# Graph attention on one Trainium2 core: key and value rows fetched one by one from the SyncE queue, 16 in three groups out of four in place of 8 in each group

## The chip, the cores and the metric

The kernel runs on one core of a Trainium2 chip. Time is device microseconds (us) of one execution. The core has five engines with an instruction stream each: TensorE (PE in the profile, PEld for its weight loads), VectorE (DVE), ScalarE (ACT), GpSimd (POOL) and SyncE (SP). SP computes nothing here: it issues DMAs. Data lie in HBM, in SBUF (128 partitions) and in PSUM, where TensorE writes.

## The reference

One graph-attention layer with residuals and two normalizations, N = 12,500 nodes, E = 212,500 edges sorted by their destination, width 128, 8 heads of 16:

```
Q, K, V = x @ WQ, x @ WK, x @ WV
Eh = edge_attr @ WE
score = exp(clip(sum over a head of (K[src] * Q[dst] / 4 * Eh), -5, 5))
wV = segment_sum(V[src] * score, dst);  Z = segment_sum(score, dst)
h = x + wV / (Z + 1e-6)
h = (h - mean over nodes) * rsqrt(var + 1e-5) * gamma + beta
out = layernorm(x + h) over the 128 columns
```

The source of an edge is random, so `K[src]` and `V[src]` are rows fetched from anywhere in a table. The destinations rise, so `Q[dst]` and the sums over a destination work on windows of 64 neighbouring nodes.

## The kernel before

**Table.** A first stage (L590 to L610, some 100 us) multiplies x by WK and WV and writes the rows of the table `kvd` to HBM: one row a node, 256 numbers (K, then V), 1 KB.

**Main loop.** The edges are cut into 1661 tiles of 128, and these into 208 groups of eight tiles (two windows of four; the last group has five). Iteration g of the loop at L671 holds steps for several groups at once, in an order written by hand. DVE runs `products` (L520, K times a projected edge feature), `both` (L503), `scores` (L527), `attn` (L570), `turned_onehot` (L461), `message` (L539, V times the score) and `onehot` (L451, L453, L454); TensorE runs the edge projection `ehqe` (L490 reads the tile `ea`, L498 follows), transposes (L511, L576) and the sums (L554); ScalarE moves PSUM results (L492, L534, L559, L582).

**How rows of the table arrive.** For each group a slot of eight tiles is filled by gathers (`gather`, L198, L199): an indirect DMA on POOL fetches 128 rows of `kvd`, one per partition, by a column of indices `srcs`. There are eight slots. When `message` has used a slot, `load_kv` (L234) gives it to a later group and appends that group's gathers to the list `queued`; all but seven go out at once, and `pace` (L206) puts one behind each of the marked DVE steps (L454, L520, the two L503, L527, L570), which POOL then waits for.

**Row loads.** In some groups the eighth tile isn't gathered by POOL. Its 128 rows come by 128 DMAs of 1 KB each from SP into a tile `byrow` (two buffers), which `products` and `message` then read in an instruction of its own (`parts`, L222). `row_groups` (L55) chooses the groups, `fill` (L216 to L219) gives each a run of successive loop iterations, and in each of these `fetch_rows` (L225) loads that many row indices from the tile `row_ids` into SP's registers (L228) and issues that many row DMAs (L232). With ROWS = 8 it takes 16 iterations for a tile, the last one three iterations (ROW_LAG) ahead of the group, and 12 tiles are filled back to back, in iterations 5 to 196.

**SP's queue.** SP executes its DMAs in order. In iteration g it issues:

```
within(load, g + 4)        # ea: 512 KB of edge features, three buffers (L420)
within(load_rel, g + 5)    # rb: two DMAs of 64 KB, three buffers (L346)
if g in fill:
    fetch_rows(*fill[g])   # L228, then L232 once for each row
```

`ea` of group g + 4 is used by `ehqe` (L490) in iteration g + 2, and `rb` of g + 5 by `turned_onehot` (L461) in iteration g + 2. The completions of SP's DMAs are counted on eight semaphores in turn, so a DMA can wait for the one eight places before it. Loads of x for the last stage (L407) follow on the same queue when the gathers have ended.

**Last stage** (L743 on): normalization, second residual and layernorm of all nodes, some 90 us.

Of the kernel before, what the change touches and what calls it, by code (L numbers as in the profile page):

```python
# [10 lines left out]
I32 = mybir.dt.int32  # L11
# [3 lines left out]
ET = mybir.EngineType  # L15

P = 128
# [4 lines left out]
U = 4  # L22
# [3 lines left out]
NX = 8  # L26
EARLY = 4
RUN = 64
ROWS = 8
FIRST_ROW = 5  # L30
ROW_LAG = 3


LAST = [3, 2]
# [2 lines left out]
def plan(N, T):  # L37

    n, r = divmod(T - sum(LAST), U)
    sizes = [U] * n + [r] * (r > 0) + list(LAST)  # L40
    assert n > 1 and len(sizes) % 2 == 0
    starts = [sum(sizes[:g]) for g in range(len(sizes))]
    cuts = list(range(0, N - 64, CH)) + [N - 64, N]
    due = {}
    thr = [0.0] * len(sizes)
    for j, c in enumerate(cuts[1:]):
        need = (c + (64 if c < N - CH else 24)) * T
        g = next((g for g, t in enumerate(starts) if t * N >= need), None)
        if g is not None:
            due.setdefault(g, []).append(j)  # L50
            thr[g] = float(c)
    return sizes, starts, cuts, due, thr


def row_groups(sizes):  # L55


    span = P // ROWS + ROW_LAG
    return [2 * g for g in range(max(FIRST_ROW + span, NX), sizes.count(U) // 2, P // ROWS)]


@with_exitstack
def gnn_kernel(
# [19 lines left out]
    nc = tc.nc  # L83
    N, D = out.shape
    T = src.shape[1]
    NW = dstb.shape[1]
    usizes, ustarts, cuts, due, _ = plan(N, T)
    NG = NW // 2
    sizes = [usizes[2 * g] + usizes[2 * g + 1] for g in range(NG)]
# [5 lines left out]
    consts = ctx.enter_context(tc.tile_pool(name="consts", bufs=1))  # L95
# [46 lines left out]
    def load_rest():  # L142
        nc.scalar.dma_start(base_i, bass.AP(tensor=dstb.tensor, offset=dstb.offset, ap=[[0, P], [1, NW]]))
        nc.scalar.dma_start(rel_i[:, :cut], dst[:, :cut])
        nc.scalar.dma_start(row_ids, rsrc)
        nc.scalar.dma_start(w_q, wq)
        nc.scalar.dma_start(w_e, we)
        nc.scalar.dma_start(srcs[:, nxg * G:cut], src[:, nxg * G:cut])
# [64 lines left out]


    by_row = {w // 2: None for w in row_groups(usizes)}
    fill = {}  # L216
    for k, g in enumerate(by_row):
        for i in range(P // ROWS):
            fill[g - ROW_LAG - P // ROWS + i] = (g, k, i)  # L219
    row_ids = consts.tile([P // ROWS, len(by_row) * ROWS], I32, name="row_ids")  # L220

    def parts(g, a, b):  # L222
        return [(a, b - 1), (b - 1, b)] if g in by_row and b == G else [(a, b)]
# [1 line left out]
    def fetch_rows(g, k, i):  # L225
        if i == 0:
            by_row[g] = rows.tile([P, 1, 2 * P], F32, name="byrow", bufs=2)
        _, ids = nc.values_load_multi_w_load_instructions(  # L228
            row_ids[i:i + 1, k * ROWS:(k + 1) * ROWS], engines=(ET.SP,), min_val=0, max_val=N - 1,
            skip_runtime_bounds_check_because="node ids")  # L230
        for p, r in enumerate(ids, i * ROWS):
            nc.sync.dma_start(by_row[g][p:p + 1, 0, :], kvd[ds(r, 1), :])  # L232
# [396 lines left out]
    for q in range(NQ):  # L629
        load_xT((q + 5) * 4 * P)  # L630
        if q == 2:
            load_rest()
        for g, a in piece.get(q, []):
            if a == 0:
                i = free.pop(0)
                kv_view(g, (i, slot(i)))
            turn_x(g, a)
        table_rows(4 * q)
        for g, a in piece.get(q, []):
            project(g, a, wide)  # L640
        k = q - first_step
        if 0 <= k < len(steps):
            for f, *a in steps[k]:
                f(*a)
# [26 lines left out]
    for g in range(NG):  # L671
        within(load, g + 4)
        within(load_rel, g + 5)
        if g in fill:
            fetch_rows(*fill[g])
# [241 lines left out]
def lay_out(x, src, dst, edge_attr_128, L0_gnn_WQ, L0_gnn_WK, L0_gnn_WV, L0_gnn_WE, L0_gnn_bn_gamma,  # L917
# [12 lines left out]

    sp = tiles(src, 0)
    rsrc = [sp[:, starts[g] + G - 1].reshape(P // ROWS, ROWS) for g in row_groups(sizes)]
    eaT = np.zeros((P, T * P), np.float32)
    eaT[:, :E] = ea.T
# [31 lines left out]
```

## Time and profile before

| | before |
|---|---|
| median of 9 runs (lowest, highest) | 2810.48 us (2788.47, 2825.11) |
| profiled execution: time, span | 2809.55 us, 2807.6 us |
| granted TensorE clock, mean of the span | 0.811 |
| busy: PE, DVE, POOL, ACT | 1923.2, 1648.9, 1588.4, 650.4 us |
| gathers of `kvd` on POOL (L199) | 1585 |
| row DMAs on SP (L232), in groups of eight (L228) | 1536, 192 |
| loads of `ea`, of `rb` | 208, 416 |
| HBM read, written | 364.57 MB, 19.63 MB |

The profile is of one execution on the chip. "busy" is the time in which an engine executes; issuing a DMA isn't counted, so SP has no busy time, and its instructions are seen in a timeline of its queue (SPq). A group of the page is a source line with its engine, operation and tiles: how often, busy us in all, mean ns of one, then the idle time of the engine ahead of it and what ended most of that. "issue" means that the engine waited for nothing the profile shows, "remote" that the semaphore's writer isn't seen. In a timeline each line is start, length, engine, source line and tiles, with the idle time before it in brackets.

### The profile page before, as it was taken

How to read it: one execution, taken by the hardware profiler on the slowest of the kernel's cores; microseconds unless marked ns; L12 is line 12 of the kernel's file. 1: busy time of each engine (PE TensorE's matmuls, PEld its weight loads, DVE VectorE, ACT ScalarE, POOL GpSimd, SP SyncE). 2: the span in 40 equal slices, each digit the busy share in tenths (PEclk: the TensorE clock that was granted, in tenths of full speed). 3: DMA queues.
4: the chain of work that ended last, by engine and by line, in shares of the span. 5: the costliest groups of instructions: out<-in, count | busy, mean ns of one | idle time of the engine just before them, and what ended most of it. 6: DMA issues, size and time to landing. Idle time of an engine off the chain costs nothing. (4 is left out here: it accounts for less than half of the span.)

```text
span 2807.6 us, 37902 instructions
## 1 busy us (share of the span) xinstructions
PE 1923.2 (68%) x9350; PEld 1264.5 (45%) x9350; DVE 1648.9 (59%) x3571; ACT 650.4 (23%) x2509; POOL 1588.4 (57%) x1681
## 2 busy tenths in 40 slices
PE   7577676766677676766665766766676766676687
PEld 5355444544344444544333434444444534444455
DVE  3346556655565666656555655656565656566585
ACT  2133222212222222222121221222222212222225
POOL 5645565655555565655554655556555655656524
PEclk9889788878877787788887878787878777878797
DMA  7644444444444444444444444444444444444453
GB/s 236 215 126 126 130 125 136 134 134 130 131 138 149 135 128 140 141 124 139 127 128 130 133 126 140 130 131 140 130 137 122 141 135 128 142 133 137 136 174 95
DMA packets 179740, 386.86 MB, mean 138 GB/s; under 512 B 41838, under 2 KB 96151, under 8 KB 179511
## 3 DMA queue, kind: packets, MB, share of 16 engines
q0 software_dynamic: 78128, 212.05, 25.9%
q1 hardware_dynamic: 98038, 169.83, 20.1%
q10 hardware_dynamic: 3345, 2.48, 0.3%
q8 instruction: 77, 1.26, 0.2%
q14 instruction: 152, 1.25, 0.1%
HBM read 364.57 MB, written 19.63 MB: 137 GB/s over the span
## 5 line engine op out<-in xcount | busy, mean ns | idle before, releaser
L199 POOL DMA_INDIRECT slot<-kvd,srcs x1585 | 1498.9, 946 | 1087.9 <-issue 330.7
L554 PE MATMUL ps_a<-msg,oh 128*128 128x136 f32 (+1 forms) x3322 | 672.1, 351 | 54.5 <-issue 52.7
L554 PEld LDWEIGHTS ps_a<-msg,oh 128*128 128x128 f32 (+1 forms) x3322 | 548.1, 212 | 159.1 <-issue 144.4
L490 PE MATMUL ps_e<-ea,w_e 128*128 128x512 f32 x832 | 455.7, 666 | 130.5 <-issue 68.4
L576 PE MATMUL ps_m<-ident,at 128*128 128x128 f32 x416 | 123.5, 388 | 461.7 <-DVE oh L454 363.9
L451 DVE TENSOR_TENSOR oh<-ps_m,rel_i 128x512 f32<-128x512 f32 x208 | 142.9, 687 | 501.1 <-remote 415.5
L520 DVE TENSOR_TENSOR p<-slot,ps_t 128x512 f32<-128x512 f32 (+1 forms) x408 | 259.5, 674 | 145.6 <-remote 119.4
L576 PEld LDWEIGHTS ps_m<-ident,at 128*128 128x128 f32 x416 | 80.4, 242 | 562.4 <-ACT xw L440 387.0
L503 DVE TENSOR_TENSOR wt<-wt,ps_q 128x512 f32<-128x512 f32 x416 | 266.1, 679 | 83.0 <-remote 54.2
L492 ACT ACTIVATE wt<-ps_e 128x512 f32<-128x512 f32 x416 | 228.0, 587 | 286.0 <-remote 184.9
L511 PE MATMUL ps_t<-ident,wt 128*128 128x128 f32 x1661 | 246.7, 294 | 67.4 <-DVE wt L503 48.3
L490 PEld LDWEIGHTS ps_e<-ea,w_e 128*128 128x128 f32 x832 | 160.6, 214 | 256.2 <-issue 228.4
L534 ACT ACTIVATE ps_m<-s 128x64 f32<-128x64 f32 x208 | 47.3, 228 | 953.6 <-issue 225.1
L527 DVE TENSOR_REDUCE s<-p 128x64 f32<-128x1024 f32 x208 | 251.3, 1208 | 0.0
L511 PEld LDWEIGHTS ps_t<-ident,wt 128*128 128x128 f32 x1661 | 207.4, 152 | 85.3 <-DVE wt L503 62.9
L539 DVE TENSOR_TENSOR msg<-slot,ps_m 128x1024 f32<-128x1024 f32 (+1 forms) x204 | 244.4, 1198 | 1.6 <-ACT hx L582 1.4
L498 PE MATMUL ps_q<-ot,q 64*128 64x512 bf16 x1248 | 201.8, 410 | 61.3 <-issue 60.3
L559 ACT ACTIVATE os<-ps_a 128x136 f32<-128x136 f32 x208 | 58.5, 281 | 708.8 <-remote 553.2
L498 PEld LDWEIGHTS <-q 64*128 64x128 bf16 x1248 | 49.6, 97 | 285.8 <-issue 260.5
L479 DVE SCALAR_TENSOR_TENSOR qr<-ps_m,q 128x128 f32<-128x128 f32 x208 | 58.2, 280 | 179.9 <-ACT hx L582 141.6
L471 PE MATMUL ps_m<-w_q,xw 128*128 128x128 f32 x416 | 107.3, 351 | 23.8 <-DVE oh L454 23.0
L461 DVE TENSOR_SCALAR ot<-rb,wiota 128x512 bf16<-128x512 bf16 x207 | 80.5, 389 | 65.4 <-DMA rb<-relT 60.8
(111 smaller groups left out, 1672.3 us busy)
## 6 DMA issues: line engine op xcount, KB each, us to landing
ea<-eaT SPq DMA_DIRECT2D x207, 512.0 KB
rb<-relT SPq DMA_DIRECT2D x414, 64.0 KB
slot<-kvd,srcs POOLq DMA_INDIRECT x1585
byrow<-kvd SPq DMA_DIRECT2D x1536, 1.0 KB
kvd<-t SPq DMA_DIRECT2D x24, 512.0 KB
slot<-xT SPq DMA_DIRECT2D x24, 256.0 KB
out<-o SPq DMA_DIRECT2D x24, 256.0 KB
hx<-xT SPq DMA_DIRECT2D x11, 512.0 KB
```

The source lines that it names most:

```text
L199: return nc.gpsimd.indirect_dma_start(out=out, out_offset=None, in_=table, in_offset=bass.IndirectOffsetOnAxis(ap=srcs[:, e:e + 1], axis=0))
L451: nc.vector.tensor_tensor(one, iota_ps[:, None, :].to_broadcast([P, n, P]), r[:, :n, None].to_broadcast([P, n, P]), op=OP.is_equal)
L490: nc.tensor.matmul(eh, w_e, EA[g][:, a:b, :].rearrange("p a b -> p (a b)"), start=True, stop=True)
L492: nc.scalar.activation(t[:, :(b - a) * P], eh, AF.Copy)
L498: nc.tensor.matmul(QE[g][h], Q3[g][r, k, :], OT[g][r, :(b - a) * P], start=(k == 0), stop=(k == 2))
L503: pace(nc.vector.tensor_tensor(t, t, QE[g][h], op=OP.mult))
L511: nc.tensor.transpose(ps[:, j, :], WT[g][h][:, j * P:(j + 1) * P], ident)
L520: step = nc.vector.tensor_tensor(PR[g][:, c:d, :], KV[g](c, d, 0), PW[g][i][:, c - a:d - a, :], op=OP.mult)
L527: pace(nc.vector.tensor_reduce(SS[g][:, :n, :], PR[g][:, :n, :].rearrange("p t (h d) -> p t h d", d=DH), axis=AX.X, op=OP.add))
L539: nc.vector.tensor_tensor(MSG[g][:, a:b, :P].rearrange("p t (h d) -> p t h d", d=DH), KV[g](a, b, P).rearrange("p t (h d) -> p t h d", d=D ...
L554: nc.tensor.matmul(AGG[g][WN if j >= n else 0:], OH[g][j], MSG[g][:, j, :], start=(j == 0), stop=(j == n - 1))
L576: nc.tensor.matmul(ps, AT[g], ident, start=True, stop=False)
```

## The change

A step now issues 16 row DMAs in place of 8, in three iterations out of four, so a tile takes eight steps. `row_steps` lists the iterations; tiles take them eight at a time, and a tile's group is three iterations after its last step. This gives 18 tiles (groups 17, 28, 38, ... 188, 198) in place of 12 (groups 24, 40, ... 200), filled in iterations 5 to 195. The row indices of 18 tiles would make rows of 288 numbers; they are folded into 24 partitions of 96, so that the tile `row_ids` keeps its width.

```diff
-ROWS = 8
+ROWS = 16
 FIRST_ROW = 5
 ROW_LAG = 3
+ROW_REST = 4
...
+def row_steps(sizes):
+    return [g for g in range(FIRST_ROW, sizes.count(U) // 2) if (g - FIRST_ROW) % ROW_REST != ROW_REST - 1]
...
 def row_groups(sizes):
-    span = P // ROWS + ROW_LAG
-    return [2 * g for g in range(max(FIRST_ROW + span, NX), sizes.count(U) // 2, P // ROWS)]
+    ends = row_steps(sizes)[P // ROWS - 1::P // ROWS]
+    return [2 * max(g + ROW_LAG, NX) for g in ends if max(g + ROW_LAG, NX) < sizes.count(U) // 2]
...
-        nc.scalar.dma_start(row_ids, rsrc)
+        nc.scalar.dma_start(row_ids, rsrc.rearrange("i (a r) -> (i a) r", a=fold))
...
+    steps_of_rows = row_steps(usizes)
     fill = {}
     for k, g in enumerate(by_row):
         for i in range(P // ROWS):
-            fill[g - ROW_LAG - P // ROWS + i] = (g, k, i)
-    row_ids = consts.tile([P // ROWS, len(by_row) * ROWS], I32, name="row_ids")
+            fill[steps_of_rows[k * (P // ROWS) + i]] = (g, k, i)
+    fold = next(a for a in (5, 4, 3, 2, 1) if len(by_row) % a == 0)
+    each = len(by_row) // fold
+    row_ids = consts.tile([P // ROWS * fold, each * ROWS], I32, name="row_ids")
...
-            row_ids[i:i + 1, k * ROWS:(k + 1) * ROWS], engines=(ET.SP,), min_val=0, max_val=N - 1,
+            row_ids[i * fold + k // each:i * fold + k // each + 1, k % each * ROWS:(k % each + 1) * ROWS], engines=(ET.SP,), min_val=0, max_val=N - 1,
```

## The prediction

> **What bounds the kernel now.** I read the page first, for the costly groups and the releasers. No engine is full: PE is busy for 68% of the span, DVE for 59%, POOL for 57%.
>
> ```profile
> L199 POOL DMA_INDIRECT slot<-kvd,srcs x1585 | 1498.9, 946 | 1087.9 <-issue 330.7
> ...
> L451 DVE TENSOR_TENSOR oh<-ps_m,rel_i 128x512 f32<-128x512 f32 x208 | 142.9, 687 | 501.1 <-remote 415.5
> ```
>
> A gather takes POOL 0.946 us, and DVE loses some 2 us a group ahead of L451 to a releaser that the profile can only call "remote". So the second view is the timeline of POOL, and then of DVE, over a stretch in mid-loop (start, length, engine, line).
>
> ```profile
> 1102.00 0.94 POOL L199 DMA_INDIRECT slot<-kvd,srcs  x1 [2.62 <-DVE oh L454]
> ...
> 1110.75 0.95 POOL L199 DMA_INDIRECT slot<-kvd,srcs  x1 [0.30 <-issue]
> 1115.22 0.94 POOL L199 DMA_INDIRECT slot<-kvd,srcs  x1 [3.52 <-DVE oh L454]
> ```
>
> ```profile
> 1106.92 1.20 DVE L539 TENSOR_TENSOR msg<-slot,ps_m 128x1024 f32<-128x1024 f32 x1
> 1113.67 0.69 DVE L451 TENSOR_TENSOR oh<-ps_m,rel_i 128x512 f32<-128x512 f32 x1 [5.54 <-remote]
> ```
>
> Eight gathers follow each other every 1.25 us (0.95 and a gap of 0.30), from 1102.0 to 1112.0. DVE is held from 1108.1 to 1113.67, and ACT's L559 is released at 1113.67 as well: 1.7 us after the last gather was issued. Then L454 lets the next gathers go at 1115.22. The cycle is 8 x 1.25 + 1.7 + 1.5 = 13.2 us. I call the stretch in which a run of gathers holds the others **the hold**. It needs no row loads: between 120 and 140 us, before the first row load, 15 gathers run and DVE is busy for 0.2 us.
>
> The third view is SP's own timeline, since SP issues the rows: first where nothing holds it, then in the cycle above.
>
> ```profile
> 1502.49 3.16 SPq L232 DMA_DIRECT2D byrow<-kvd  x8
> 1505.74 0.36 SPq L420 DMA_DIRECT2D ea<-eaT  x1
> 1506.20 1.10 SPq L346 DMA_DIRECT2D rb<-relT  x2
> 1508.51 3.15 SPq L232 DMA_DIRECT2D byrow<-kvd  x8
> ```
>
> ```profile
> 1104.38 9.97 SPq L232 DMA_DIRECT2D byrow<-kvd  x8
> 1114.45 0.36 SPq L420 DMA_DIRECT2D ea<-eaT  x1
> 1114.90 1.10 SPq L346 DMA_DIRECT2D rb<-relT  x2
> 1117.21 9.82 SPq L232 DMA_DIRECT2D byrow<-kvd  x8
> ```
>
> A free step of SP (row ids, eight rows, ea, two rb) takes 1508.51 - 1502.49 = 6.02 us. In the held cycle the same step takes 1117.21 - 1104.38 = 12.83 us, because the eight rows take 9.97 us in place of 3.16. The fourth view is what SP waits for between 190 and 2662 us (us in total, times, longest).
>
> ```profile
> SPq L420 <- PE ps_e L490: 16.7, 6, 8.9
> SPq L232 <- DMA byrow<-kvd: 15.5, 36, 0.8
> SPq L346 <- DMA relT<-relrow: 12.2, 1, 12.2
> ```
>
> All its waits there add up to 94.6 us, of which 22.4 us are at L232 (a lane or an earlier load) and 72 us for buffers of ea and rb. The loads of row ids run from 190.3 to 2656.1 us, 192 times: 2465.8 / 191 = 12.91 us for a step. So SP, though it computes nothing, works for 96% of the loop; 6.02 us of a step is work, 0.50 us waiting and 6.39 us loss to the hold. It is sometimes late already, by the waits of all engines:
>
> ```profile
> PE ps_e L490 <- DMA ea<-eaT: 61.7, 14, 10.5
> DVE ot L461 <- DMA rb<-relT: 60.8, 13, 11.0
> ```
>
> The reader is to see two limits side by side: a run of gathers makes the cycle about 13 us, and SP needs 12.91 us for its step.
>
> **The change, part by part.** *Gathers.* By the built order of instructions 18 groups have seven gathers in place of 12: 1585 - 6 = 1579. Each is worth 1.25 us of a run if the run sets the cycle: 6 x 1.25 = 7.5 us gained. If SP sets it, the gain goes into POOL's idle time. I take 0 for my forecast and 7.5 us for the first rival.
>
> *DVE.* Six more groups split products and message. From the rows by form: products 548 + 280 in place of 679 ns, message 1073 + 276 in place of 1208 ns, together 0.29 us a group, 1.7 us in all, hidden in the holds (5.54 us above); 1.7 us if that cover goes.
>
> *Row loads.* 18 x 128 = 2304 in place of 1536, so 768 more, in 144 steps of 16 in place of 192 steps of eight. Eight rows take 3.16 us where nothing holds SP: (3.16 - 0.23) / 7 = 0.42 us a row (its two register instructions and the 0.228 us of the median DMA).
>
> ```profile
> L232 SPq DMA_DIRECT2D byrow<-kvd x1536: 2/228/1421, 191.5 to 2662.2; - x192
> ```
>
> A load of row ids has a median of 0.976 us, 1.03 with its gap, and there are 48 fewer. Free work added: 768 x 0.42 - 48 x 1.03 = 322.6 - 49.4 = 273 us, over the same groups (steps 5 to 195 in place of 5 to 196). What is moved: in iteration g the queue has ea of group g + 4, rb of g + 5, then the rows; so 16 rows stand ahead of the next ea and rb, 3.4 us more even when free, and PE (L490) and DVE (L461) wait for those. The rows themselves are asked for later: they are issued three groups ahead, and ea only two, so ea is late first. The two byrow buffers make no wait: a tile is used three groups after its last step and its buffer is wanted again 10 groups or more after that step.
>
> *The price of an added row* is not shown for a queue of 16. From below it is 0.42 us. From above it is the mean of before: a step's rows take 12.91 - 0.50 - (6.02 - 3.36) = 9.75 us, 1.22 us a row. I take 0.42, since the hold lasts as long as the run of gathers and the runs don't grow; time that SP adds to the cycle comes after the run, where the 6.02 us step lies. With it SP's step is, in the mean over 191 groups, (144 x 9.38 + 47 x 1.6) / 191 = 7.47 us of work (1.6 us is a step without rows: ea, two rb and their gaps), to which the hold adds its 6.39.
>
> [...]
>
> **The sum.** 273 us of work, of which the 72 us that SP waits for buffers take their share: 273 - 72 = 201 us, nothing for the gathers, nothing for DVE. The profiled execution took 2809.55 us (span 2807.6), 0.9 us under the median of nine runs, so one forecast serves for both: 2809.55 + 201 = **3010 us**. By steps: 7.47 + 6.39 + 0.12 (the waits at L232 that stay) = 13.98 us in place of 12.91, times 191 = 204 us.
>
> **Rivals.** *1, not slower: the hold eases.* Place: SP's rows within the run of gathers. If a held SP is only slow because nothing presses it, the rows fit into the cycle and one gather less shortens six runs: 2809.55 - 7.5 + 0 = 2802 us. It decides from the point where SP's loss falls from 6.39 to under 12.91 - 7.47 = 5.4 us a step. For it: after the last rows, from 2664.05 to 2677.06 us (L527 to L527), a cycle without rows takes 13.0 us as well, so today's rows cost little. Against: the late ea and rb, and SP's 96%.
>
> *2, much slower: the mean price.* If each added row pays 1.22 us, since the queue fills the held stretches too: 768 x 1.22 - 48 x 2.2 (an id load at the same stretch) - 72 = 759 us, 3569 us. For it: the mean step, 12.91 us, is that of the stretch at 1104, so a free step is the exception. Against: no gather is added, and what SP adds lies behind a run.
>
> *3, faster: a shorter run escapes the hold.* DVE is held from 6 us after a run's start. With POOL idle, after 2692 us, a group takes 7.5 us (L527 at 2696.2 and 2703.7); if six more groups fell from 12.9 to 7.5, that is 32 us: 2777 us. Against: a run of seven still lasts 8.75 us.
>
> *4, the change doesn't do what it says.* The built order shows 18 runs of seven, 18 splits, 24 x 96 row ids, and no other engine's order changed: left at nothing.
>
> **How the numbers follow.** SP as the bound at about 0.42 us a row, 2870 to 3200 us: 0.58. Rival 1: 0.21. Rival 2, or a price towards it, over 3200 us: 0.09. Rival 3: 0.12. About 0.5% (14 us) is what a measurement of this kernel tells from no change. Faster by more: rival 3 and a little of rival 1, 0.14. Within: the rest of rival 1, 0.19. Slower: 0.67. The range goes from 2795 us, to hold rival 1, to 3200 us; it leaves out most of rival 3 and rival 2, some 2 in 10. The forecast's own range is 2870 to 3200.
>
> **What would show it.** Right: the id loads of successive groups with rows stand over 14 us apart; SP's buffer waits (L420, L346) near nothing; PE's wait for ea and DVE's for rb grown from 61.7 and 60.8 us to some 200 us together or more; POOL's idle time up by about as much, in longer gaps between runs of the same 1.25 us. Wrong: eight added rows that cost nothing while those two waits stay near 60 us (rival 1); rows at over a microsecond each after the run has ended (rival 2); several cycles near 7.5 us around the groups with seven gathers (rival 3). The forecast fails first if the hold's length depends on what SP issues, which no row here separates.

## The result, and the profile after

| | before | after |
|---|---|---|
| median (lowest, highest) | 2807.06 us (2788.47, 2825.11), 31 runs | 3013.95 us (3002.4, 3033.27), 10 runs |
| profiled execution: time, span | 2809.55, 2807.6 us | 3027.42, 3025.6 us |
| granted TensorE clock | 0.811 | 0.798 |
| ratio, 95% interval | | 1.0748 (1.0722 to 1.0774) |

The change makes the kernel 207 us slower by the medians. The two profiled executions, on which the readings below rest, are 218 us apart. First the page's groups of after, as in the first view of before (the last columns are the idle time ahead of the group and its main releaser):

```profile
L204 POOL DMA_INDIRECT slot<-kvd,srcs x1579 | 1493.9, 946 | 1312.3 <-DVE oh L462 373.8
L459 DVE TENSOR_TENSOR oh<-ps_m,rel_i 128x512 f32<-128x512 f32 x208 | 142.8, 686 | 473.9 <-remote 419.7
```

A gather costs what it did, and ahead of this line DVE loses to "remote" what it did (415.5 us before). POOL's idle time is up from 1087.9 to 1312.3 us, by 224 us, about as much as the span (218 us). The timelines of POOL and DVE in mid-loop show the same run and the same hold:

```profile
1502.92 0.94 POOL L204 DMA_INDIRECT slot<-kvd,srcs  x1 [3.73 <-DVE oh L462]
...
1511.67 0.94 POOL L204 DMA_INDIRECT slot<-kvd,srcs  x1 [0.30 <-issue]
1515.94 0.95 POOL L204 DMA_INDIRECT slot<-kvd,srcs  x1 [3.32 <-DVE oh L462]
...
1526.27 0.94 POOL L204 DMA_INDIRECT slot<-kvd,srcs  x1 [1.87 <-DVE msg L547]
```

```profile
1514.39 0.69 DVE L459 TENSOR_TENSOR oh<-ps_m,rel_i 128x512 f32<-128x512 f32 x1 [5.34 <-remote]
...
1524.32 0.35 DVE L469 TENSOR_SCALAR ot<-rb,wiota 128x512 bf16<-128x512 bf16 x1 [3.92 <-DMA rb<-relT]
...
1534.86 0.29 DVE L528 TENSOR_TENSOR p<-byrow,ps_t 128x128 f32<-128x128 f32 x1 [6.49 <-DMA byrow<-kvd]
```

Eight gathers at 1.25 us, a hold that ends at 1514.39, 1.5 us after the run (1511.67 + 1.25), the next gathers at 1515.94: a cycle of 13.0 us, like those of before. What follows is new. DVE waits 3.92 us for `rb` and, ten microseconds later, 6.49 us for the rows themselves. SP's timeline says why:

```profile
1504.55 14.39 SPq L240 DMA_DIRECT2D byrow<-kvd  x16
1519.03 0.41 SPq L428 DMA_DIRECT2D ea<-eaT  x1
1520.18 1.48 SPq L354 DMA_DIRECT2D rb<-relT  x2
1523.10 10.57 SPq L240 DMA_DIRECT2D byrow<-kvd  x16
```

Sixteen rows fill the whole hold and more; `rb` is issued only at 1520.18 us. Over the loop, by the waits of all engines:

```profile
DVE ot L469 <- DMA rb<-relT: 478.2, 77, 16.1
...
PE ps_e L498 <- DMA ea<-eaT: 369.4, 67, 14.6
...
DVE p L528 <- DMA byrow<-kvd: 40.1, 11, 6.5
```

The first two were 60.8 and 61.7 us; the third had no line in before. SP's own waits between 190 and 2860 us are down to 78.5 us, of which this is most:

```profile
SPq L240 <- DMA byrow<-kvd: 30.6, 65, 1.1
SPq L240 <- DMA relT<-relrow: 20.4, 3, 13.5
SPq L428 <- PE ps_e L498: 8.6, 3, 6.3
```

SP hardly waits for a buffer any more (27 us of the 78.5, where before had 72): it is the bound, and the others wait for it. Last, the row that gives its step, the loads of row ids (number, then duration min/median/max in ns, then first and last start in us):

```profile
L236 SPq TENSOR_LOAD <-row_ids x144: 5/1429/1474, 189.6 to 2867.7; - x144
```

They span 191 iterations from the first step to the last, 190 intervals: (2867.7 - 189.6) / 190 = 14.10 us a group, where before had 12.91. Between loads of successive groups with rows it is more than 14 us in 91 of 96 cases, as the prediction asked; the groups that rest make up for it.

### The profile page after: what moved, and what is told of

It is laid out like the page before. It is cut to its first block, busy times and chain, and to the rows that moved or that the text cites. A ratio compares the mean times of both kernels' runs of the same rounds, so it can differ in the third digit from the quotient of the medians.

```text
span 3025.6 us, 40194 instructions
## 1 busy us (share of the span) xinstructions
PE 1928.3 (64%) x9350; PEld 1246.3 (41%) x9350; DVE 1646.5 (54%) x3583; ACT 658.6 (22%) x2509; POOL 1583.5 (52%) x1675
## 5 line engine op out<-in xcount | busy, mean ns | idle before, releaser
L204 POOL DMA_INDIRECT slot<-kvd,srcs x1579 | 1493.9, 946 | 1312.3 <-DVE oh L462 373.8
L498 PE MATMUL ps_e<-ea,w_e 128*128 128x512 f32 x832 | 503.1, 733 | 405.1 <-DMA ea<-eaT 369.4
L562 PE MATMUL ps_a<-msg,oh 128*128 128x136 f32 (+1 forms) x3322 | 644.9, 343 | 16.0 <-issue 14.3
L562 PEld LDWEIGHTS ps_a<-msg,oh 128*128 128x128 f32 (+1 forms) x3322 | 530.5, 206 | 114.3 <-issue 98.6
L459 DVE TENSOR_TENSOR oh<-ps_m,rel_i 128x512 f32<-128x512 f32 x208 | 142.8, 686 | 473.9 <-remote 419.7
L498 PEld LDWEIGHTS ps_e<-ea,w_e 128*128 128x128 f32 x832 | 170.4, 227 | 551.7 <-issue 541.1
L469 DVE TENSOR_SCALAR ot<-rb,wiota 128x512 bf16<-128x512 bf16 x207 | 78.5, 379 | 511.5 <-DMA rb<-relT 478.2
L519 PE MATMUL ps_t<-ident,wt 128*128 128x128 f32 x1661 | 229.5, 282 | 69.5 <-DVE wt L511 43.5
L535 DVE TENSOR_REDUCE s<-p 128x64 f32<-128x1024 f32 x208 | 251.3, 1208 | 0.0
L519 PEld LDWEIGHTS ps_t<-ident,wt 128*128 128x128 f32 x1661 | 196.5, 146 | 77.6 <-DVE wt L511 49.6
```

The source lines that it names most:

```text
L204: return nc.gpsimd.indirect_dma_start(out=out, out_offset=None, in_=table, in_offset=bass.IndirectOffsetOnAxis(ap=srcs[:, e:e + 1], axis=0))
L459: nc.vector.tensor_tensor(one, iota_ps[:, None, :].to_broadcast([P, n, P]), r[:, :n, None].to_broadcast([P, n, P]), op=OP.is_equal)
L498: nc.tensor.matmul(eh, w_e, EA[g][:, a:b, :].rearrange("p a b -> p (a b)"), start=True, stop=True)
L519: nc.tensor.transpose(ps[:, j, :], WT[g][h][:, j * P:(j + 1) * P], ident)
L535: pace(nc.vector.tensor_reduce(SS[g][:, :n, :], PR[g][:, :n, :].rearrange("p t (h d) -> p t h d", d=DH), axis=AX.X, op=OP.add))
L562: nc.tensor.matmul(AGG[g][WN if j >= n else 0:], OH[g][j], MSG[g][:, j, :], start=(j == 0), stop=(j == n - 1))
```

## The experiments

**Theory S:** SP's work is added up per group, the hold takes its share of SP's time on top, and from the point where the sum exceeds the cycle of the gathers, `ea` and `rb` are late. **Rivals:** B, it is the burst of 16 rows ahead of `ea` and `rb` that costs, not the sum; and G, it is something else in the change (18 split groups, fewer gathers), so that the rows don't matter.

The runs were made in four groups, each on one chip with the kernel before beside it. One plain fact has to be known ahead of all: in the first three groups the kernel before took 2152 to 2156 us, in the fourth 2804 us. What differs in the traces is the hold, as e5 shows.

**e1 to e4: the rows taken away, halved, spread.** e1 is the changed kernel and e2 the kernel before, each with one DMA for a tile's 128 rows:

```diff
-        _, ids = nc.values_load_multi_w_load_instructions(...)
-        for p, r in enumerate(ids, i * ROWS):
-            nc.sync.dma_start(by_row[g][p:p + 1, 0, :], kvd[ds(r, 1), :])
+        if i == 0:
+            nc.sync.dma_start(by_row[g][:, 0, :], kvd[k * P:(k + 1) * P, :])
```

> The changed kernel, but each byrow tile is filled by one DMA of 128 neighbouring rows of the table (so the eighth tile of 18 groups holds the wrong rows) and no row ids are loaded: SP's step falls to the 1.6 us of ea and rb, all other engines' work stays. Theory S (the sum of SP's issue time is the limit of the changed kernel): the 207 us go, and with them the 122 us that PE and DVE waited for ea and rb before, as far as nothing else takes their place: 2690 to 2800 us, and no waits for ea and rb in the loop. Theory H (SP's time is harmless, the slower cycle comes from the gathers' hold or from splitting more groups): stays near 3014.

> The same for the kernel before: 12 tiles, each by one DMA (wrong rows). Theory S says that SP was on the edge already, so some of the 122 us of waits for ea and rb go: 2700 to 2805 us; the distance to e1_after_one_dma is then what six gathers are worth when SP is free, 7.5 us by 1.25 us each, in any case under 35. If SP had been free in the kernel before: 2807 within 0.5%.

e3 is the changed kernel with 16 rows in two iterations of four (12 tiles, as before, but in bursts):

```diff
-ROW_REST = 4
+ROW_REST = 2
```

> 16 rows a step, but in two groups out of four: 1536 rows and 12 tiles as before, 96 loads of row ids in place of 192. Theory S counts the sum: 1536 rows as before, ids 96 x 1.43 = 137 in place of 192 x 0.976 = 187 us, so 50 us less work: 2760 to 2810 us. Theory B (what costs is that 16 rows stand in a burst ahead of the next ea and rb, not their sum): most of the loss stays, two thirds of 207, near 2945.

e4 is the kernel before with four more rows of the table in each step (752 in all), into a tile that nothing reads:

```diff
+            if k * 16 + i >= 4 and p % 2:
+                ...
+                nc.sync.dma_start(again[0][p:p + 1, k % 4, :], kvd[ds(r, 1), :])
```

> The kernel before with 12 rows in every step: each second row is fetched once more into an unused tile, 752 more row DMAs, no longer burst than 12, the same 12 tiles and 1585 gathers. Theory S: 752 x 0.42 = 316 us of work less some 50 to 72 of waits: 3050 to 3075 us, about 40 to 60 above the changed kernel, since the ids stay at 192 loads. Theory B: 12 in a row are between 8 and 16, under 2950. Rival of the mean price (1.22 us a row): 3600.

| run | median us | ratio to before (2152.94 us), 95% interval |
|---|---|---|
| e1 | 2144.18 | 0.9959 (0.9943 to 0.9974) |
| e2 | 2153.4 | 0.9997 (0.9981 to 1.0014) |
| e3 | 2151.59 | 0.9996 (0.9981 to 1.001) |
| e4 | 2153.97 | 0.9995 (0.9977 to 1.0012) |

All four expectations had been reckoned from 2807 us, and their times couldn't be tested. The distance from e2 to e1, set at 7.5 us for six gathers, is 9.2 us. What the four do show: where the kernel takes 2153 us, row loads on SP are free, 1536 of them or 2288, in bursts or not.

**e5 and e6: the changed kernel itself, and e4 again.** No edit.

> The changed kernel as it is, since the kernel before took 2153 us beside the four runs so far and 2807 beside the result. Theory S with the hold (SP is short of time only where a run of gathers holds it): if the kernel before takes about 2807 us here, 3014 again; if it takes about 2153, no hold, SP has time to spare, POOL's gathers are the bound and six fewer are worth 6 x 1.25 = 7.5 us: 2145. Theory S without the hold (16 rows are too much for SP in any case): some 7% over the kernel before in either case.

> The kernel before with 12 rows in every step (752 more row DMAs, the same gathers), as e4_twelve_in_each. If the kernel before takes about 2807 us here: theory S 3050 to 3075 us, by the sum of SP's work; theory B (the burst of 16 is what costs) under 2950; the hold alone, 2807. If the kernel before takes about 2153: the same as it within 0.3%.

e5 took 2148.5 us, ratio 0.9975 (0.996 to 0.999): beside this before the change is faster by a quarter of a per cent. e6 took 2157.17 us, 0.9999 (0.9982 to 1.0016). Two rows show what is different at 2153 us: SP's register instructions at the row loads, first in e5 and then in after of the result.

```profile
L240 SPq FUSED_REGOPS  x2304: 37/37/51, 133.5 to 1982.2; - x192
```

```profile
L240 SPq FUSED_REGOPS  x2304: 2/37/1397, 191.1 to 2877.5; - x192
```

Such an instruction, by its name arithmetic on SP's registers alone, takes 37 to 51 ns in e5, and up to 1397 ns in after. In the trace of after the held stretches show SP's instructions, whatever they are, passing at about 0.70 us each or for two: from 1506.45 to 1513.59 us their starts, or those of two together, are 0.70 to 0.78 or some 1.4 us apart. A row is three instructions (2304 each of FUSED_REGOPS, MOVE and DMA). In e5 nothing is held: among its longest waits, down to 15.2 us in all, none of DVE or ACT is for "remote", where after has 502.3 us of them on DVE and 937.6 us on ACT; ahead of L459 DVE is idle for 0.0 us, where after has 473.9; and in its timeline POOL issues gathers every 1.25 us without a break.

```profile
1505.04 0.95 POOL L204 DMA_INDIRECT slot<-kvd,srcs  x1 [0.30 <-DVE rz L574]
1506.30 0.94 POOL L204 DMA_INDIRECT slot<-kvd,srcs  x1 [0.30 <-issue]
```

Nor is there a wait of DVE or ACT for "remote" among the longest of e2, e4, f2 and f3, down to 6.4 us or less in all, or among the few longest of e1 and f1; in f1 SP's register instructions take 37 to 51 ns as well. e3 and e6 I count with them by their times, 2151.59 and 2157.17 us. So without the hold the bound is POOL, as the waits of e5 say (`products` waits for gathered rows), although `rb` and `ea` are already late now and then:

```profile
DVE p L528 <- DMA slot<-kvd,srcs: 262.6, 118, 5.9
...
DVE ot L469 <- DMA rb<-relT: 50.2, 18, 4.6
...
PE ps_e L498 <- DMA ea<-eaT: 28.1, 13, 3.7
```

Six gathers fewer are then worth about what the prediction put them at: 2155.68 - 2148.5 = 7.2 us (2 to 9 by the interval), against 6 x 1.25 = 7.5 us.

**f1, f2: SP made the bound without the hold.** Since the hold was not to be had there, 24 more row DMAs at fixed addresses were put into each of iterations 9 to 195, into a tile that nothing reads; f1 is the kernel before with them, f2 the changed one.

```diff
+        if 9 <= g < 196:
+            ...
+            for p in range(24):
+                nc.sync.dma_start(again[p:p + 1, g % 4, :], kvd[g * 60 + p:g * 60 + p + 1, :])
```

> The kernel before with 24 more row DMAs in each group from 9 to 195, from fixed rows of the table into an unused tile: they cost SP some 0.28 us each (the 0.228 of the DMA and a gap), 6.7 us a group, about what the hold took from SP in the traces of before (6.39). Nothing holds PE, DVE or ACT. Theory S, where the kernel before takes 2153 us: SP's step goes from 6.02 to 12.7 us and is over the 9.71 us cycle of the gathers, so SP is the bound: 2153 + 187 x 3.0 = 2715 us (2600 to 2800). If a full queue of SP is harmless: 2153.

> The changed kernel with the same 24 DMAs a group. Theory S: the change's own work is now paid in full, as in the result. By the free stretches of e5_after_again a step of 16 takes 9.99 us to the next and a step without rows adds 1.72, so (144 x 9.99 + 47 x 1.72) / 191 = 7.95 us a group against 6.02: 187 x 1.93 = 361 us over f1_before_sp_loaded. If the row loads cost nothing by themselves and the result came from the hold alone: 7 us under f1_before_sp_loaded.

f1 took 2811.74 us (ratio 1.3062, 1.3029 to 1.3095), f2 3177.18 us (1.4775, 1.4742 to 1.4808). f1 lies over its range: one fixed row DMA costs SP 0.295 us (24 in 7.05 us), more than I had put in. The difference is what was asked for: 365.4 us, where 361 were expected. With SP the bound and nothing held, the changed step costs that much more than the step before. By its parts it is 768 x 0.41 = 315 us for the rows, and for the ids 144 x 1.48 - 192 x 1.03 = 15 us (a load of 16 ids has a median of 1.44 us in these runs, of eight 0.98 us, each with 0.05 us of gap): 330 us. SP's own waits over the loop place some 22 of the other 35: 66.3 us in f2 against 44.7 in f1, with 30.0 us of the added rows for `ea` that f1 doesn't have (46 times, about as often as a group rests). The bound shows in the waits of f2 as in after, only longer; the last line is SP's own:

```profile
DVE ot L469 <- DMA rb<-relT: 1212.9, 178, 10.0
PE ps_e L498 <- DMA ea<-eaT: 1117.9, 171, 10.3
...
SPq L688 <- DMA ea<-eaT: 30.0, 46, 1.2
```

**f3: more tiles.** The changed kernel with a rest in one iteration of eight (21 tiles, 1576 gathers).

```diff
-ROW_REST = 4
+ROW_REST = 8
```

> The changed kernel with rows in seven groups of eight: 21 tiles, 1576 gathers. Where there is no hold, SP's mean step is (7 x 9.99 + 1.72) / 8 = 8.96 us, still under the 9.7 us of the gathers' cycle: 3 x 1.25 = 4 us faster than the changed kernel, 2144 to 2146, if nothing else comes late; no gain if the one rest in eight is too little for ea and rb, which then show as waits. Where there is the hold (before 2807): a third more above before than the changed kernel, over 3060.

2144.4 us, ratio 0.997 (0.9957 to 0.9982): as expected. Without the hold 21 tiles by SP are no worse than 18; that they are better isn't shown, since the interval overlaps that of e5. The waits for `ea` and `rb` are twice those of e5, 64.0 and 89.5 us, and cost nothing that can be seen.

**g1, g2, g3: with the hold.** In the fourth group the kernel before took 2804.23 us (7 runs, 2794.41 to 2814.36), as in the result.

> The same kernel as e1 (the changed kernel, each byrow tile by one DMA of 128 neighbouring rows, no loads of row ids, so wrong rows in the eighth tile of 18 groups), once more, in case this run meets the hold that e1 did not. With the hold (the kernel before near 2807 us): theory S gives 2770 to 2802 us, since SP drops out as a bound and the runs of gathers alone set the cycle; if the added time of the changed kernel comes from the split groups or their gathers instead, 2950 us or more. Without the hold (the kernel before near 2153 us): 2144 us again, ratio 0.994 to 0.998.

g3 took 2686.96 us, ratio 0.9573 (0.9537 to 0.9609). Rival G falls: the splits and the gathers of the change are all there, and the time is under that of before. PE and its weight loads wait for `ea` by 4.1 us in all, and `rb` isn't among DVE's longest waits, down to 16.3 us; SP waits for buffers instead. The row of `ea`'s loads in g3, and who waited for them, then SP's waits:

```profile
L425 SPq DMA_DIRECT2D ea<-eaT x208: 327/334/562, 61.9 to 2596.1; - x104
...
  PE ps_e L495: 1.9, 1
```

```profile
SPq L425 <- remote: 1205.7, 94, 31.1
SPq L425 <- PE ps_q L503: 439.4, 33, 16.3
```

But 2687 us is 83 us under the lower end of what S gave. I had taken the cycle of before for that of the gathers alone. It was not: before was paying for its own row loads, 2804.23 - 2686.96 = 117 us with the six gathers in it (some 7 us). That this is near the sum of its waits for `ea` and `rb`, 61.7 + 60.8 = 122.5 us, is no rule: PE and DVE can wait at the same time, and in place of other waits. In after the sum is 847.6 us, and g3 is only 327 us under it. From the first to the last load of `ea`, g3 needs (2596.1 - 61.9) / 207 = 12.24 us a group, before 12.78 and after 13.84.

> The changed kernel with the 24 fixed row DMAs a group of f2, but each byrow tile by one DMA of 128 neighbouring rows of the table, with no loads of row ids (so 18 groups compute with wrong rows in their eighth tile). SP's step is then 1.7 + 24 x 0.295 = 8.8 us, under the 9.7 us of a cycle without hold. If the price of f2 lies in the single rows: 2143 to 2155 us where no hold occurs, over 1000 us less than f2. If it lies in the split of products and message in 18 groups or in the 24 added DMAs: well over 2300 us. Where the hold occurs: SP's step is 8.8 us plus what the hold takes of it, as in the kernel before, so near 2807 us or somewhat over.

g2 has the edits of e1 and of f2 together. It took 2857.76 us, ratio 1.0187 (1.0111 to 1.0264). That is 171 us over g3 for 187 x 7.05 = 1318 us of added SP work: most of it fits into the time in which g3's SP waits for buffers, and the rest is past the point where SP becomes the bound (PE waits 337 us for `ea` again, DVE 429 for `rb`). It also speaks against a rival that isn't named above, that the added transfers load the DMA engines: g2 moves 4488 single rows of 1 KB, after 2304, and g2 is 156 us faster. A group of g2 takes 13.27 us, from the first to the last of the 24 DMAs, less the last 8 us of them, over 186:

```profile
L685 SPq DMA_DIRECT2D t<-kvd x4488: 2/250/1508, 237.3 to 2713.2; - x196
```

> The kernel before with 12 rows in each group's step (the eight of before, and four more rows of the table into a tile that nothing reads) and the 24 fixed row DMAs a group that f1 has, so that SP sets the time where no hold occurs. It issues 752 more rows than f1, nearly as many as the changed kernel adds, but evenly. Theory S (only the sum of SP's work counts): f1's 2811.74 us plus 752 x 0.41 = 308 us, 3120 us (3080 to 3160); 57 us under f2's 3177.18, of which the longer loads of 16 row ids explain about as much. Theory B (a run of 16 rows ahead of ea and rb costs by itself, evenly spread rows don't): clearly nearer f1, under 3000 us. Where the hold occurs, S gives more than 3120 us.

```diff
+            if k * 16 + i >= 4 and p % 2:
+                ...
+        if 9 <= g < 196:
+            ...
+            for p in range(24):
```

g1 took 3854.13 us, ratio 1.3747 (1.3693 to 1.3801). With the hold S had only a lower end, which held. B asked for under 3000 us, but from f1's time without the hold, and no run with the hold has f1's edit alone; so g1 speaks against B and doesn't settle it. Spread rows are paid for too: from g2 to g1 SP has 2288 x 0.41 + 192 x 1.03 = 1136 us more, and the time is 996 us longer. The waits of g1 are those of a kernel that SP paces in every group, and the loads of row ids give its step:

```profile
DVE ot L467 <- DMA rb<-relT: 1823.3, 182, 12.4
PE ps_e L496 <- DMA ea<-eaT: 1665.3, 181, 12.1
...
DVE oh L457 <- remote: 55.0, 8, 23.2
...
L230 SPq TENSOR_LOAD <-row_ids x192: 663/977/1002, 189.0 to 3704.7; - x192
```

The wait of DVE for "remote" is 419.7 us in after. DVE is hardly caught by the hold any more, presumably since it already waits for `rb` in that time; ACT still is (1022.1 us over all its lines).

## Why the prediction was right, and where its terms were off

The forecast was 3010 us and the median is 3013.95 us. The mechanism stands: g3 takes SP's single rows away, and the late `ea` and `rb` go, and with them 327 us of the changed kernel's time (3013.95 - 2686.96; 1.0748 against 0.9573 of the kernel before beside each). Its signs came too: id loads over 14 us apart, the two waits at 847.6 us together where 200 or more were asked for, POOL's idle time up by 224 us. The closeness of the two numbers is partly luck, because three terms were off and cancel. All are per step, for 191 steps:

| term | forecast | measured | from |
|---|---|---|---|
| work of SP's step | 7.47 us | 7.78 us | (144 x 9.76 + 47 x 1.71) / 191; 9.76 is 6.02 + 8 x 0.41 + 0.46 |
| SP's waits | 0.12 us | 0.41 us | 78.5 / 191 |
| loss to the hold | 6.39 us | 5.91 us | 14.10 - 7.78 - 0.41 |
| step | 13.98 us | 14.10 us | loads of row ids |

- **Work.** The 0.42 us of a row is about right (free of the hold, eight rows take 3.13 us in e5, 0.41 between them; 16 take 7.02 us in f2, 0.45 between them). The step that failed is "48 fewer at 1.03 us": I let a load of 16 ids cost what a load of eight does. It takes 1.429 us instead of 0.976, and so the id loads are 15 us more and not 49.4 us less, 65 us in all. That the time grows with the number of ids is what I missed: 0.453 us for eight more, 57 ns each.
- **SP's waits.** The 72 us for buffers that were to be swallowed were largely swallowed, some 27 us are left. But the waits at the rows rose from 22.4 to 51.0 us: 30.6 us for earlier rows, 65 times where it had been 36 (presumably because 16 rows in a burst come round to the same completion semaphore more often: in the trace of after SP's 3022 DMAs name eight of them, 377 to 379 times each, and each of the 2304 row DMAs waits for the one it names), and 20.4 us in three waits for another transfer. 55 us were mis-sized here.
- **The hold's loss.** I carried 6.39 us over as a constant. It is 5.91 us in after, (18.41 - 14.53 - 0.66) = 3.2 us in g1 and (13.27 - 8.77 - 0.63) = 3.9 us in g2: step, less free work, less SP's waits. (g1's step: id loads from 189.0 to 3704.7 us over 191; its work 6.02 + 752 x 0.41 / 191 + 187 x 7.05 / 191; its waits 125.2 us. g2's work 7.05 + 1.72, its waits 116.5 us over 186.) DVE's waits for "remote" at `onehot` and `products` together shrink the same way: 534.9 us before, 458.9 in after, 225.5 in g2, 59.9 in g1. I take it that where SP delays the others, gathers come later and fill less of the cycle, so that less of SP's work falls into the hold; that is argued, not shown. In g2 a fixed row is one instruction, not three, which may matter as much; no run separates the two. This gave back 0.48 x 191 = 92 us.
- **The sum.** 338 us of work in place of 273, less 17 in place of 72 for waits, less 92 for the hold: 229 us against 201. By the steps it is (14.10 - 12.91) x 191 = 227; the profiled executions are 218 us apart, the medians 207.
- **"ea is late first, and the byrow buffers make no wait".** In the waits of after the rows are late too: 40.1 us, 11 times, with POOL's gathers behind them (38.3 us). The distance of three groups that I counted on is worth nothing once SP itself is late by more than it. In e5, with no hold, nobody but POOL (3.0 us) waits for the tile.
- **The gathers at nothing.** Fits where SP is the bound, since POOL's idle time grew, but no run with the hold tests it alone. Without the hold their price is 7.2 us (e5).
- **Rival 1 (2802 us)** was mispriced: with the rows out of the way the time is 2687 us. Its point of decision, a loss of 5.4 us a step, stands at 12.24 - 7.78 = 4.5 us by g3's cycle and the measured work; after has 5.91. With no hold at all the loss is nothing, and it is rival 1 that happens (0.9975).
- **Rival 2** falls: 768 rows and their ids cost 218 us of span in all, 0.28 us a row. **Rival 3** falls the other way round: by the spacing of L527 and L535 between groups 8 and 195, cycles under 8.5 us went from 24 to 13, and those over 14.5 us from 33 to 51. The median cycle only went from 13.08 to 13.34 us. The change costs by making some cycles long, not all of them.

**What stays open.** Why a run of gathers holds the other engines in some runs and not in others isn't shown. A low clock isn't what makes it: f1 has 0.802 and no hold (register instructions of 37 to 51 ns), before 0.811 and a hold (up to 1410 ns). Theory B was tried only where SP was loaded further; whether a burst costs something of its own at after's load, with the hold, isn't separated, since e4 met no hold. And of the fixed and the per-instruction part of the hold's loss nothing is settled.

## What to carry to other kernels

Before adding issue work to a queue, add up its step and compare it with the cycle of everything else without that queue's work: what lay under cost little or nothing here (e4 at 0.9995; g2, 171 us for 1318 us of work), what lay over was paid nearly in full or more (f2, 365 us for 330; g1, 996 for 1136). Waits of other engines for that queue's transfers call for this sum and don't replace it: 122.5 us of them went with a price of 117 us before, but 153.5 us in f3 with none. And a condition that no line of the code sets, such as the hold, can decide the sign: the same change is 7.5% slower with it and 0.25% faster without, so look for its mark in a trace before carrying a verdict elsewhere.

## What the runs showed of the hardware

- The same kernel before takes 2153 us or 2807 us. With the hold, SP's register instructions of 37 ns take up to 1.4 us while gathers run back to back, and DVE and ACT wait for a releaser that isn't seen (624.3 and 995.7 us before); without it they take 37 to 51 ns (e5, f1), and beside gathers at the same 1.25 us none of the longest waits of e5, down to 15.2 us in all, is of that kind.
- Where nothing is held, SP issues a 1 KB row at a register's address in 0.41 to 0.45 us (three instructions; eight in 3.13 us in e5, in 3.19 us in f1, 16 in 7.02 us in f2), at a fixed address in 0.295 us (one; 24 in 7.05 us in f1). A load of eight ids takes 0.976 us (before), of 16 1.43 to 1.44 us (after, e5, f2).
